# Cross-attention in turns of four heads, with the program's ends in another form

## The chip, the cores and the metric

The kernel runs on one core of one Trainium2 chip. A core has a matrix engine (PE; its weight loads are listed apart as PEld), a vector engine (DVE), an activation engine (ACT), a general engine (POOL) and a queue that issues the transfers (SP). Each takes its own instructions in the order in which the program lists them, and the engines wait for one another by semaphores. The metric is the device time of one execution in microseconds (us), lower is better.

## The reference

One decoder block on `x` of 8 sequences x 224 rows x 512, with a context of 8 x 750 x 384:

```python
# self-attention: 16 heads of 64, RMS norm in front, normed q and k, tanh soft clamp
x = layernorm(x + self_attention(x))
# cross-attention: 16 heads of 64
q = split_heads(x @ Wq); k = split_heads(context @ Wk); v = split_heads(context @ Wv)
sim = einsum('bhid,bhjd->bhij', q, k) * SCALE
out = einsum('bhij,bhjd->bhid', softmax(sim), v)
x = layernorm(x + out @ Wo + bo)
# feed-forward with ternary weights and 8-bit activations, inner width 2048
x = layernorm(x + ffn(x))
```

## The kernel before, in words

The 1792 rows of `x` lie in 14 tiles of 128 rows (`NX`). Three stages follow one another: self-attention, cross-attention, feed-forward. Inside a stage the order of each engine's instructions is written out by hand: what the program calls first, the engine does first. The change is mostly in the middle stage.

**Units.** Cross-attention is done in 64 units: 8 sequences b times 8 pairs of heads hp. For each unit:

- `scores` multiplies keys by queries (12 matmul calls into 6 PSUM tiles of 125 x 448, `sc_c`, line 1067). ACT copies each tile to SBUF (`cpT`, line 1075). DVE keeps an elementwise maximum (`cm`, line 1077), folds it once more (`cmx`, line 1081).
- `across` turns column maxima and the column sums of the unit before into rows: two transposed reductions (`mx_r`, line 1095), four small copies between partition groups (`mx_s`, line 1102), reductions and a reciprocal, three more small copies (`mx_n`, line 1124). All of it is on DVE.
- `negated_maxima` spreads the result by a transpose into a PSUM tile (`mx_b`, line 1131).
- `exponentials` subtracts the maxima on DVE (two instructions of 125 x 1344, line 1141), takes the exponential on ACT (two, line 1149) and sums on POOL (lines 1151 to 1153, into `csm`).
- `weighted` multiplies the exponentials by the values (`ov_c`, line 1161); `normalise` scales by the reciprocal sums (`rc_c`, line 1174, and line 1178) into `oT`.

**Products.** Keys and values are made for four heads at once by seven block products, `half_products` (line 244), which needs three PSUM accumulators x, z and w. Its part up to the first `yield` runs the products x, z, x, w, x; its rest runs w and x again. Between two products of one accumulator ACT has to copy the first out: `m1` (line 266), then `c11` (272), `u2` (274), `c22` (279), `u4` (282); POOL adds `m1` to `c11` and `u4` to `c22` (lines 288 and 289). The rest ends with a DVE add (`c21`, line 294) and an ACT copy (`c12`, line 298). In the trace key products bear the names `k_x`, `k_z`, `k_w` (line 1028), value products `v_x`, `v_z`, `v_w` (line 1034).

**The loop** (lines 1239 to 1290) has one round for each unit n. In a round PE does: scores of n; weighted values of n-1; the first part of the products; the queries of n+1 (`mm_q`, line 1043); the rest of the products. The products are those of values in one round and those of keys in the next. ACT does in a round: the 6 copies of scores; the five copies of the first part of the products; the copy of the queries; the two exponentials; `c12`. DVE does: the maxima, `across`, the spread, the two subtractions, `c21`, `normalise`.

**Beside it.** A generator, `weight_steps`, prepares the ternary weights of the feed-forward: ACT sums and rounds, DVE clamps, transfers through SP; nearly every unit takes one of its 38 steps. `transpose_x` makes the queries' input of the next sequence, `sum_context` the block sums of its context on POOL. `cross_finish` projects a finished tile of rows by `xattn_Wo` (`mm_co`, line 232) and adds it. `norm_at` lists at which unit the layer norm of finished tiles takes a step. All PSUM tiles but `ov_c` come from one ring of seven banks.

**The end of the program** is the last tile of the feed-forward: `contract` (16 matmuls of 128 x 512), `add` (add, statistics, one power on POOL), `store` (scaling and the transfer out).

Of the kernel before, what the change touches and what calls it, by code (L numbers as in the profile page):

```python
# [64 lines left out]
def decoder_block(ctx: ExitStack, tc: tile.TileContext, a: dict, out: bass.AP):  # L65
# [249 lines left out]
    with tc.tile_pool(name="a_sb", bufs=2) as sb, tc.tile_pool(  # L315
# [366 lines left out]

        for i in range(4):
            square(i)
# [183 lines left out]
    def quantise_x(i):  # L868

        r = quant.tile([P, DIM], F32, name="xq_r")  # L870
        nc.scalar.activation(r, x[i], AF.Identity, bias=rounder, scale=x_qs[:, i, :])
        q = quant.tile([P, DIM], BF16, name="xq_q")
        nc.scalar.activation(q, r, AF.Identity, bias=unrounder)
        xqTs[i] = quant.tile([P, KD, P], BF16, name="xqT", bufs=3)
        nc.sync.dma_start_transpose(out=xqTs[i], in_=q)

    with tc.tile_pool(name="c_sb", bufs=2, reuse_waits="tile") as sb, tc.tile_pool(
# [17 lines left out]
        csm = sb.tile([P, 2, S], F32, name="csm", bufs=1)  # L895
# [158 lines left out]
        def scores(kT, qT):  # L1054

            pT = sb.tile([CT, 2, NCT, S], F32, name="cpT")
            m2 = sb.tile([CT, 2, 2, S], F32, name="cm2", bufs=1)
# [25 lines left out]
            )  # L1083
            return pT

        def across(first, last):
# [4 lines left out]
            kinds = slice(1 if last else 0, 1 if first else 2)  # L1091

            quarter = sb.tile([P, 2, 2 * NB], F32, name="mx_r", bufs=1)
            for k, y, op in ((0, mx, ALU.max), (1, csm, ALU.add))[kinds]:
                nc.vector.tensor_reduce(
                    quarter[:, k], y.rearrange("p j (b c) -> p (j b) c", c=Q32), AX.X, op,
# [3 lines left out]
            side = sb.tile([Q32, 2, 2 * NB, P // Q32], F32, name="mx_s", bufs=1)  # L1100
# [4 lines left out]
            res = sb.tile([P, 4, NB, 1], F32, name="mx_n")  # L1105
            if not last:
                nc.vector.tensor_reduce(
                    res[:Q32, 1:3, :, 0].rearrange("p j b -> p (j b)"), side[:, 0], AX.X,
                    ALU.max, negate=True,
                )  # L1110
            if not first:
                tot = sb.tile([Q32, 2, NB], F32, name="mx_t", bufs=1)
                nc.vector.tensor_reduce(
                    tot.rearrange("p j b -> p (j b)"), side[:, 1], AX.X, ALU.add
                )
                nc.vector.reciprocal(res[:Q32, 0:4:3, :, 0], tot)
# [12 lines left out]
        def negated_maxima(res):  # L1129
# [3 lines left out]
                res[:, 1:3].rearrange("p j b o -> p (j b) o").to_broadcast([P, 2 * NB, Q32]),  # L1133
# [3 lines left out]
        def exponentials(pT, nm):  # L1137

            psum = csm[:CT]
            for j in range(2):  # L1140
# [7 lines left out]
                )  # L1148
                nc.scalar.activation(pT[:, j], pT[:, j], AF.Exp)  # L1149
# [5 lines left out]
        def weighted(hp, pT, v):  # L1155

            ov = ps_ov.tile([P, S], F32, name="ov_c")
            for ct in range(NCT):
                for j in range(2):
                    h0, hq = j * DH, (2 * hp + j) % QH  # L1160
                    nc.tensor.matmul(  # L1161
                        ov[h0 : h0 + DH, :],
                        lhsT=v[:, ct, hq * DH : (hq + 1) * DH],
                        rhs=pT[:, j, ct, :],
                        start=(ct == 0),
                        stop=(ct == NCT - 1),
                    )
            return ov

        def normalise(b, hp, ov, res):  # L1170
            rc = sb.tile([P, S], F32, name="rc_c", bufs=1)
            for j in range(2):
                half = slice(j * DH, (j + 1) * DH)
                nc.vector.transpose(
                    rc[half], res[half, 3 * j].to_broadcast([DH, NB, Q32])
                )
            c = b % 2 * S
            nc.vector.tensor_tensor(oT[:, hp, c : c + S], ov, rc, ALU.mult)
# [15 lines left out]

        norm_at = {}
        for n, i0, i1 in ((4 * NPAIR + 2, 0, 7), (7 * NPAIR + 1, 7, NX - 3)):
# [4 lines left out]
        norm_at[6 * NPAIR] = (quantise_x, 0)  # L1203
        norm_at[6 * NPAIR + 1] = (quantise_x, 1)
# [3 lines left out]
        units = [(b, hp) for b in range(B) for hp in range(NPAIR)]  # L1208
        steps = weight_steps()
        kq, vs, outs = {}, {}, {}  # L1210
# [310 lines left out]
```

## Time and profile before

| | |
|---|---|
| median of 3 runs | 1646.17 us (1645.54 to 1646.76) |
| the profiled execution | 1645.14 us, its span 1643.4 us |
| PE, PEld | busy 1623.3 us, 1147.3 us |
| DVE, ACT, POOL | busy 1336.5 us, 976.8 us, 901.4 us |
| granted PE clock | 0.999 |
| DMA queue q1 | 147.93 MB, 29.2% of 16 engines' span |
| cross-attention, first scores to first matmul of the feed-forward | 508.62 to 1491.17 us |

The span runs from the first to the last instruction; the time of the execution has some 1.7 us around it. "Busy" of PE counts matmuls whose ends are modelled and which overlap, so what a matmul costs in a dense stretch is read from the distance of starts, not from its mean duration. Matmuls of 32-bit numbers appear as two records each: the 12 calls of `scores` are 24 records. In the lists by time a line gives start, duration, engine, source line, operation, tiles and shapes, a count where alike instructions were merged, and in square brackets the engine's idle time before, with what ended it. "Pitch" below means the distance from one start to the next.

### The profile page before, as it was taken

What the parts mean: (1) busy time and instruction counts of PE and PEld (TensorE: products, weight loads), DVE (VectorE), ACT (ScalarE), POOL (GpSimd) and SP (SyncE); (2) the same over time, 40 slices, a digit from 0 to 9 for tenths busy, and PEclk for the clock granted to TensorE, in tenths of its full rate; (3) what the DMA queues carried; (4) which work ended last, traced back from release to release, by engine and by line L of the source; (5) the groups of instructions that cost most, each with busy time, mean ns of one, the idle gap of its engine ahead of it and who ended that gap; (6) DMA issues with size and microseconds to landing.
All of it is one profiled execution on the core that took longest, in us unless ns stands there. A gap on an engine that the chain in (4) does not pass through costs nothing.

```text
span 1643.4 us, 27371 instructions
## 1 busy us (share of the span) xinstructions
PE 1623.3 (99%) x9844; PEld 1147.3 (70%) x9858; DVE 1336.5 (81%) x2813; ACT 976.8 (59%) x1774; POOL 901.4 (55%) x792
## 2 busy tenths in 40 slices
PE   8999999999999999999999999999999999999998
PEld 4777666767747877876876876877877777874443
DVE  3999787878866887886986986898987787987877
ACT  4766555646515766765775775666665565655663
POOL 5785565554523665655565565565665565653244
PEclk9999999999999999999999999999999999999999
DMA  7005232312305333321332232232221131122343
GB/s 256 39 39 193 65 119 87 105 49 74 91 32 177 128 123 119 126 95 48 111 114 81 84 114 83 76 115 83 60 74 47 41 100 44 49 104 39 65 90 103
DMA packets 140071, 149.67 MB, mean 91 GB/s; under 512 B 41120, under 2 KB 106144, under 8 KB 137504
## 3 DMA queue, kind: packets, MB, share of 16 engines
q1 hardware_dynamic: 139936, 147.93, 29.2%
q8 instruction: 78, 1.28, 0.3%
q14 instruction: 57, 0.47, 0.1%
HBM read 122.47 MB, written 16.78 MB: 85 GB/s over the span
## 4 chain that ended last, share of the span: by engine, by line
PE 85%; DVE 9%; ACT 3%; issue 2%; POOL 0%; DMA 0%; POOLq 0%; SPq 0%; ACTq 0%; DVEq 0%
PE sc_c L1067 8%; PE ov_c L1161 8%; PE mm_o L629 6%; PE k_x L1028 6%; PE mm_co L232 6%; PE mm_f L1322 6%; PE v_x L1034 5%; PE mm_q L1043 5%; PE mm_v L503 5%; PE q_x L437 5%; PE k_w L1028 4%; PE v_w L1034 4%; PE ov_a L596 3%; PE sc_a L527 3%; PE q_w L437 2%; PE k_z L1028 2%
## 5 line engine op out<-in xcount | busy, mean ns | idle before, releaser
L1151 POOL TENSOR_TENSOR csh<-cpT 125x672 f32<-125x672 f32 x128 | 207.7, 1623 | 161.4 <-DVE cpT L1141 123.5
L1075 ACT COPY cpT<-sc_c 125x448 f32<-125x448 f32 x384 | 173.8, 562 | 76.3 <-PE sc_c L1067 74.8
L167 POOL TENSOR_TENSOR nm_i<-nm_q,mhalf 128x28 f32<-128x28 f32 x32 | 154.6, 4831 | 96.0 <-DVE nm_q L484 95.9
L1149 ACT ACTIVATE cpT<-cpT 125x1344 f32<-125x1344 f32 x128 | 169.1, 1323 | 48.1 <-DVE cpT L1141 40.2
L1141 DVE TENSOR_TENSOR cpT<-cpT,mx_b 125x1344 f32<-125x1344 f32 x128 | 193.2, 1550 | 2.2
L1067 PE MATMUL sc_c<-cqT,ckT 64*125 64x224 f32 x1536 | 172.5, 360 | 3.8 <-DVE cpT L1141 2.9
L1067 PEld LDWEIGHTS sc_c<-cqT,ckT 64*125 64x125 f32 x1536 | 143.1, 184 | 36.9 <-issue 22.5
L1161 PE MATMUL ov_c<-cpT,cv 125*64 125x224 f32 x1536 | 159.4, 357 | 0.0
L1161 PEld LDWEIGHTS ov_c<-cpT,cv 125*64 125x64 f32 x1536 | 104.8, 137 | 47.2 <-issue 11.2
L1077 DVE TENSOR_TENSOR cm<-sc_c,cpT 125x448 f32<-125x448 f32 x128 | 73.8, 619 | 73.9 <-ACT cpT L1075 73.9
L1043 PE MATMUL mm_q<-xT,xattn_Wq 128*128 128x224 f32 x512 | 107.3, 352 | 0.0
L1153 POOL TENSOR_TENSOR csm<-csm,csh 125x224 f32<-125x224 f32 x128 | 97.6, 763 | 10.0
L503 PE MATMUL mm_v<-wv,xnT 128*128 128x512 f32 x224 | 100.4, 592 | 0.0
L1043 PEld LDWEIGHTS mm_q<-xT,xattn_Wq 128*128 128x128 f32 x512 | 94.3, 190 | 8.1
L252 ACT ACTIVATE pr<-sc_a 128x448 f32<-128x448 f32 x120 | 57.9, 535 | 69.5 <-PE sc_a L527 69.4
L1152 POOL TENSOR_TENSOR csm<-csh 125x224 f32<-125x224 f32 x128 | 93.7, 732 | 10.0
L629 PE MATMUL mm_o<-attn_Wo,oT 128*128 128x512 f32 (+1 forms) x224 | 98.7, 594 | 0.0
L232 PE MATMUL mm_co<-xattn_Wo,coT 128*128 128x512 f32 (+1 forms) x256 | 98.6, 594 | 0.0
L1322 PE MATMUL mm_f<-ternary,xqT 128*128 128x512 bf16 x435 | 97.6, 379 | 0.7
L551 DVE TRANSPOSE_TENSOR_REDUCE sm_q<-pr 128x28 f32<-128x896 f32 x64 | 70.6, 1104 | 23.5 <-ACT pr L252 23.0
L1322 PEld LDWEIGHTS <-xqT 128*128 128x128 bf16 x448 | 43.8, 98 | 53.2 <-issue 0.6
L232 PEld LDWEIGHTS mm_co<-xattn_Wo,coT 128*128 128x128 f32 (+1 forms) x256 | 40.3, 177 | 50.6 <-issue 49.3
(211 smaller groups left out, 3723.9 us busy)
## 6 DMA issues: line engine op xcount, KB each, us to landing
xw<-w_sums SPq DMA_DIRECT2D x64, 320.0 KB, 3.0
w_slot<-qk_sums SPq DMA_DIRECT2D x22, 512.0 KB, 3.7
w_stage<-w_gateT SPq DMA_DIRECT2D x8, 1024.0 KB, 5.2
w_stage<-w_upT SPq DMA_DIRECT2D x8, 1024.0 KB, 5.3
w_stage<-w_downT SPq DMA_DIRECT2D x8, 1024.0 KB, 5.6
xw<-xattn_Wk SPq DMA_DIRECT2D x32, 192.0 KB, 2.6
xw<-xattn_Wv SPq DMA_DIRECT2D x32, 192.0 KB, 2.5
tern<-w_t SPq DMA_DIRECT2D x24, 256.0 KB, 2.0
```

The costliest lines, as they stand in the source:

```text
L232: nc.tensor.matmul(mm[row : row + m, :], lhsT=oT[:, k, at : at + m], rhs=w[:, k, :], start=(k == 0), stop=(k == NPAIR - 1),)
L503: nc.tensor.matmul(mm, lhsT=xnT[:, k, at : at + P], rhs=wv[:, k, c * 512 : (c + 1) * 512], start=(k == 0), stop=(k == KD - 1),)
L629: nc.tensor.matmul(mm[row : row + lhsT.shape[-1], :], lhsT=lhsT, rhs=wo[:, hp, :], start=(hp == 0), stop=(hp == NPAIR - 1),)
L1028: nc.tensor.matmul(mm, lhsT=w, rhs=c, start=start, stop=True, skip_group_check=True)
L1043: nc.tensor.matmul(mm, lhsT=xwq[:, k, hp * P : (hp + 1) * P], rhs=xT[:, k, :], start=(k == 0), stop=(k == KD - 1),)
L1067: nc.tensor.matmul(sc[j][:, i, :], lhsT=kT[h0 : h0 + DH, ct * CT : (ct + 1) * CT], rhs=qT[h0 : h0 + DH, :], start=True, stop=True,)
L1075: nc.scalar.copy(pT[:, j, 2 * c2 : 2 * c2 + 2, :], sc[j])
L1141: nc.vector.tensor_tensor(pT[:, j], pT[:, j], nm[:CT, j] .rearrange("p (o q) -> p o q", o=1) .to_broadcast([CT, NCT, S]), ALU.add,)
L1149: nc.scalar.activation(pT[:, j], pT[:, j], AF.Exp)
L1151: nc.gpsimd.tensor_tensor(half, pT[:, j, 0:3], pT[:, j, 3:6], ALU.add)
L1161: nc.tensor.matmul(ov[h0 : h0 + DH, :], lhsT=v[:, ct, hq * DH : (hq + 1) * DH], rhs=pT[:, j, ct, :], start=(ct == 0), stop=(ct == NCT - 1),)
L1322: nc.tensor.matmul(mm, lhsT=xqTs[i][:, k, :], rhs=w[:, k, cols], start=(k == 0), stop=(k == KD - 1),)
```

## The change

Two units make a turn of four heads. In turn d PE does: the weighted values of both units of turn d-1 side by side (one PSUM bank); the scores of both units of d; the queries of the first unit of d+1; the first part of the value products of d; the queries of the second unit; the rest of the value products; the key products of d+1. `across` is called once for four heads; the transposed reduction of the maxima has moved into `scores`, once for each unit, and that of the sums is one of double width. `negated_maxima`, the subtraction (now `less_maxima`) and the exponentials are called for each unit: those of the first between the two parts of the value products, those of the second between the two parts of the key products. One weight step is taken in a turn, and one more where a tile is finished; what is left of them follows the loop, and so does the loading of the ternary weights. At the start of the program 20 matmuls on a cleared tile are added. At its end the last tile is contracted in two halves of 256 columns, and each half is added, measured, scaled and stored by itself.

```diff
+        cleared = sb.tile([P, P], F32, name="cleared", bufs=1)
+        nc.vector.memset(cleared, 0.0)
+        warm = ps_mm.tile([P, P], F32, tag="mm", name="warm")
+        for _ in range(20):
+            nc.tensor.matmul(warm, lhsT=cleared, rhs=cleared, start=True, stop=True)
+
         for i in range(4):
             square(i)
...
-        def scores(kT, qT):
+        def scores(kT, qT, quarter):
...
             nc.vector.tensor_tensor(
                 mx[:CT], m2[:, :, 0, :], m2[:, :, 1, :], ALU.max
             )
+
+            nc.vector.tensor_reduce(
+                quarter, mx.rearrange("p j (b c) -> p (j b) c", c=Q32), AX.X, ALU.max,
+                apply_transpose=True,
+            )
             return pT
...
-            kinds = slice(1 if last else 0, 1 if first else 2)
...
+            kinds = slice(2 if last else 0, 2 if first else 4)
+            if not first:
                 nc.vector.tensor_reduce(
-                    quarter[:, k], y.rearrange("p j (b c) -> p (j b) c", c=Q32), AX.X, op,
+                    quarter[:, 2:].rearrange("p u n -> p (u n)"),
+                    csm.rearrange("p u j (b c) -> p (u j b) c", c=Q32), AX.X, ALU.add,
                     apply_transpose=True,
                 )
...
-                nc.vector.reciprocal(res[:Q32, 0:4:3, :, 0], tot)
+                for j in range(2):
+                    nc.vector.reciprocal(
+                        res[:Q32, 3 * j, :, 0].rearrange("p (u b) -> p u b", u=2), tot[:, :, j]
+                    )
...
-        def weighted(hp, pT, v):
+        def weighted(d, pTs, v):
 
-            ov = ps_ov.tile([P, S], F32, name="ov_c")
-            for ct in range(NCT):
+            ov = ps_ov.tile([P, 2, 256], F32, name="ov_c")
+            for u in range(2):
+                for ct in range(NCT):
...
+        def quantise_first(i):
+            quantise_x(
+                i,
+                sb.tile([P, 2, 2, S], F32, tag="cm2", name="xq_r", bufs=1)
+                .rearrange("p i j q -> p (i j q)")[:, :DIM],
+                sb.tile([P, PIECE], BF16, tag="w_t", name="xq_q", bufs=1)[:, :DIM],
+            )
...
+        for d in range(ND):
+            b, hp = units[2 * d]
+            more = d + 1 < ND
+            if d > 0:
+                ov = weighted(d - 1, pTs, v)
+            quarter = sb.tile([P, 4, 2 * NB], F32, name="mx_r", bufs=1)
+            pTs = [scores(kT[:, u], qTs[u], quarter[:, u]) for u in range(2)]
+            res = across(quarter, d == 0, False)
+            qTs = []
+            if more:
+                qTs.append(turn_queries(d + 1, 0))
+            v, values = turn_values(d)
+            next(values)
+            nm = negated_maxima(res, 0)
+            if more:
+                qTs.append(turn_queries(d + 1, 1))
+            less_maxima(pTs[0], nm)
+            exponentials(pTs[0], 0)
+            for _ in values:
                 pass
...
+            if d > 0:
+                normalise(d - 1, ov, res)
             for f in late:
                 f()
             late.clear()
+            if more:
+                kT, keys = turn_keys(d + 1)
+                next(keys)
+            nm = negated_maxima(res, 1)
+            less_maxima(pTs[1], nm)
+            exponentials(pTs[1], 1)
+            if more:
+                for _ in keys:
+                    pass
...
+            weight_step()
...
             if spare:
                 cross_finish(spare.pop(0))
+                for f in late:
+                    f()
+                late.clear()
+                weight_step()
...
         cross_finish(NX - 3)
...
+        cross_project(NX - 2, 0, NPAIR - 2)
+        cross_project(NX - 1, 0, NPAIR - 2)
+        ov = weighted(ND - 1, pTs, v)
+        quarter = sb.tile([P, 4, 2 * NB], F32, name="mx_r", bufs=1)
+        normalise(ND - 1, ov, across(quarter, False, True))
         for i in (NX - 2, NX - 1):
-            cross_project(i, NPAIR - 1, NPAIR)
+            cross_project(i, NPAIR - 2, NPAIR)
             cross_add(i)
...
-        def contract(i):
+        def contract(i, parts=1):
...
+            for c, dn in enumerate(dns[i]):
+                for k in range(HID // P):
+                    nc.tensor.matmul(
+                        dn,
+                        lhsT=hqT[:, k, :],
+                        rhs=wd[:, k, c * n : (c + 1) * n],
...
+        def finish_end():
+
+            _, deq = deqs.pop(END)
+            halves = [x[END][:, c : c + DIM // 2] for c in range(0, DIM, DIM // 2)]
+            st = stat.tile([P, 2, 6], F32, name="ln_st2", bufs=1)
+            for c, (y, dn) in enumerate(zip(halves, dns.pop(END))):
+                nc.vector.scalar_tensor_tensor(y, dn, deq, y, ALU.mult, ALU.add)
+                nc.vector.bn_stats(st[:, c, :], y)
+            mv, rs = ln_mv[:, END, :], ln_rs[:, END, :]
+            nc.vector.bn_aggr(mv, st)
+            nc.vector.tensor_scalar(ln_ve[:, END, :], mv[:, 1:2], LN_EPS, None, ALU.add)
+            rsqrt(rs, ln_ve[:, END, :])
+            store(nc.vector, 1)
+            for c, y in enumerate(halves):
+                nc.vector.tensor_scalar(
+                    y, y, mv[:, 0:1], rs, ALU.subtract, ALU.mult
+                )
+                nc.sync.dma_start(
+                    out=x_out[END * P :, c * DIM // 2 : (c + 1) * DIM // 2], in_=y
+                )
...
-        contract(END)
+        contract(END, 2)
         add(NX - 2)
-        add(END)
-        store(nc.vector, 2)
+        finish_end()
```

The layer norm's steps of `norm_at` move by up to two units, so that two of them fall into one turn, and the first two row tiles quantised for the feed-forward (`quantise_first`) use the rooms of `cm2` and `w_t` instead of rooms of their own.

## The prediction

> **What bounds the kernel now.** First the page's busy shares and its chain of waits:
>
> ```profile
> PE 1623.3 (99%) x9844; PEld 1147.3 (70%) x9858; DVE 1336.5 (81%) x2813; ACT 976.8 (59%) x1774; POOL 901.4 (55%) x792
> PE 85%; DVE 9%; ACT 3%; issue 2%; POOL 0%; DMA 0%; POOLq 0%; SPq 0%; ACTq 0%; DVEq 0%
> ```
>
> PE is busy all the time and is most of the chain, so the time falls only where PE's stream gets shorter, and rises with every hole in it. Then the list by time of a clean stretch of cross-attention, PE:
>
> ```profile
> 1421.60 2.54 PE L1067 MATMUL sc_c<-cqT,ckT 64*125 64x224 f32 x24
> 1424.06 2.49 PE L1161 MATMUL ov_c<-cpT,cv 125*64 125x224 f32 x24
> 1426.48 0.92 PE L1034 MATMUL v_x<-xw,ctx_odd 128*125 128x128 f32 x6
> 1431.17 1.68 PE L1043 MATMUL mm_q<-xT,xattn_Wq 128*128 128x224 f32 x8
> 1432.69 1.47 PE L1034 MATMUL v_w<-xw,ctx_odd 128*125 128x128 f32 x12
> 1435.40 1.78 PE L1067 MATMUL sc_c<-cqT,ckT 64*125 64x224 f32 x16
> ```
>
> Scores start at 1421.60 and 1435.40: 13.80 us for a unit with value products, 13.53 for one with key products, 27.34 for two. The pieces follow each other without a hole: scores 2.47, weighted values 2.42, value products 4.69 + 2.71, queries 1.51 (pitches). The first and last product records of a unit take about 0.10 more than the others: that is what a change of tile shape costs, four times in 27.34. The other two engines of the same unit, ACT and then DVE:
>
> ```profile
> 1422.71 2.72 ACT L1075 COPY cpT<-sc_c 125x448 f32<-125x448 f32 x6
> 1427.50 0.48 ACT L266 COPY cm<-v_x 125x384 f32<-125x384 f32 x1 [2.08 <-PE v_x L1034]
> 1433.14 2.72 ACT L1149 ACTIVATE cpT<-cpT 125x1344 f32<-125x1344 f32 x2
> 1435.77 0.46 ACT L298 COPY cv<-v_x 125x384 f32<-125x384 f32 x1
> 1436.51 0.97 ACT L1075 COPY cpT<-sc_c 125x448 f32<-125x448 f32 x2 [0.28 <-PE sc_c L1067]
> ```
>
> ```profile
> 1424.14 1.16 DVE L1077 TENSOR_TENSOR cm<-sc_c,cpT 125x448 f32<-125x448 f32 x2 [0.54 <-ACT cpT L1075]
> 1427.67 0.60 DVE L1095 TRANSPOSE_TENSOR_REDUCE mx_r<-csm 128x14 f32<-128x448 f32 x1
> 1428.31 0.76 DVE L1102 COPY mx_s<-mx_r 32x28 f32<-32x28 f32 x4
> 1429.72 0.98 DVE L1124 COPY mx_n<-mx_n 32x21 f32<-32x21 f32 x3
> 1430.73 0.66 DVE L1131 STREAM_TRANSPOSE mx_b<-mx_n 128x448 f32<-128x448 f32 x1
> 1431.43 3.02 DVE L1141 TENSOR_TENSOR cpT<-cpT,mx_b 125x1344 f32<-125x1344 f32 x2
> 1434.36 0.55 DVE L294 TENSOR_TENSOR cv<-v_w,cu 125x384 f32<-125x384 f32 x1
> ```
>
> ACT always waits for PE here (2.08 us before the copy of the first product), and gets to the exponentials only after the first part of the products. DVE runs without a hole from the first maximum (2.54 us after the scores start) to the end of the subtractions (10.22 us later). Exponentials (ACT goes on 1.41 us after the last subtraction), the copy of c12 and the first copies of scores close the ring in about 13.5 us: it only just fits into a unit. Where it doesn't, PE shows a hole:
>
> ```profile
> 1177.65 1.86 PE L1067 MATMUL sc_c<-cqT,ckT 64*125 64x224 f32 x14 [1.29 <-DVE cpT L1141]
> ```
>
> I went through all 64 distances between scores, less `mm_co` and the transposes: ten units (6, 7, 14, 15, 38, 39, 44 to 47) are longer than 13.53 or 13.81, by 0.8 to 2.0 us, together 13.8 us.
>
> **The turn, PE's part.** Removed: two of four changes of tile shape, 0.2 us; the matmuls stay. Without a hole a turn takes 27.14. With the first scores of a turn as zero, from the pitches above and those of the key unit before (first part 0.63, 1.26, 0.63, 1.27, 0.63): scores 2 x 2.47 and a change of shape to 5.04; queries to 6.55; first part of values 4.58, to 11.13; queries to 12.64; rest of values 2.61, to 15.25; k_x to 15.88; k_z to 17.14. There the second k_x wants to start, and it may do so only once ACT has copied the first (m1).
>
> **What stands before that copy.** ACT's order is now: 12 copies of scores, queries, five copies of the values' first part, queries, *both exponentials of the first unit*, c12 of the values, then m1 of the keys. Before, only c12 and the next scores queued behind exponentials, and the weighted values stood between. So the keys wait for DVE, whose subtractions of the first unit come after the maxima of both units and a wider `across`. Pitches, from the lines above and their neighbours: two units of maxima and folded reduction (1.07 + 1.18 + 0.71 + 0.57 each) 7.06; the sums' reduction at double width 1.10, from the same shape in self-attention:
>
> ```profile
> L551 DVE TRANSPOSE_TENSOR_REDUCE sm_q<-pr 128x28 f32<-128x896 f32 x64 | 70.6, 1104 | 23.5 <-ACT pr L252 23.0
> ```
>
> four copies 0.90 (0.80, and the 32x56 copy of self-attention is 215 ns where a clean one here is 190); two reductions 0.47 (0.12 + 0.23, each wider by about 0.06); two reciprocals 0.52; three copies 1.01; spread 0.70; subtractions 2.93. Sum 14.69. ACT has no arrears when scores start (below), so the first maximum stays at 2.54 and the subtractions end at 17.23. ACT then needs 1.41 to reach c12, 0.45 for it, 0.47 for m1, and PE takes it up some 0.06 later: 19.62. **The hole is 19.62 - 17.14 = 2.5 us in every turn.** Nothing covers it: PE keeps its order, and the next product but one needs the same accumulator.
>
> Behind it: x, w, x follow in 2.53; the second w waits for c22, whose copy ends about 0.74 after w where the x between takes 0.63 (queries stood there before), 0.1; the last two 2.52 and a change of shape bring the weighted values to 24.86 and the next scores to 29.70. **A turn takes 29.70, 2.36 more than two units.**
>
> What else was moved, and what hides it. DVE behind 17.23: c21 0.47, two transposes 1.3 (64x448, 640 ns in self-attention), the multiply 0.62 (128x448 there), spread 0.70, subtractions 2.93: 23.3. The second unit's exponentials start after u4 at 22.84 and end at 25.5; its weighted values start at 27.28, so 1.8 us of slack take in a weight clamp (0.74). POOL's sums of that unit end near 30.5, sum_context (0.92 each) or the bias (1.27) before 33, and the double reduction comes at 39. ACT ends c12 at 26.0 and has until 30.8 for a weight step (1.92 + 0.19, or 1.24 + 1.21) and a transpose copy; with a finished tile there are 6.87 us of `mm_co` more for the second step. The two norm steps in a turn (1.2 each, DVE) fall where DVE is idle, 23.9 to 32.2. The PSUM ring is read seven tiles back: the eleventh score tile waits at most 0.1 for its maximum. SP loads the block weights after their last product: 3 us to land, used over 10 us later. Ternary loads (9.2 us each) now come after the last values, with `mm_co` of 17 us and the last weighted values in front of the feed-forward. All that I cost at nothing.
>
> Bounds of the hole: the three copies take 0.56 where POOL is idle and 1.36 beside it, the four 0.80 and 1.64 (groups at 1470 and 1214 us). All clean: 2.0. All beside POOL: 3.7. I take 2.5, since POOL's add for c22 falls at 11.94 to 12.94, on the three copies, and leaves the four free. A row that I have not seen (double reduction, two-unit copies) could take another 0.8 off: 1.2 at the least.
>
> **The ends.** Warm matmuls: 40 records. In the list of the start PE is idle until 6.31; eight 128-column records then take 1.87 us, and at 11.92 eight take 1.00. If all the added ones run slow (0.234) they end near 10.5, if they turn fast after 5 us near 8. The first transposes come 1.5 to 4 late, the products behind gain about 0.9 for each eight. Between -1.0 and +1.0; I take -0.2. The last tile: adds and statistics of the second half cost 0.75 + 0.69 less, about by half, 0.6; the last scaling is two instructions of some 0.3 for one of 0.55; 32 half-width matmuls 0 to 0.3 more. Between -0.9 and +0.3; I take -0.5. The last weighted values are followed by a multiply (0.62 and a signal) that nothing covers now: +0.75. `quantise_first` shares the room of `w_t`, so ACT waits for a 2.0 us transfer in two turns: 0 to +3, I take +1.
>
> **Sum.** 31 turns with keys x 2.36 = +73.2; the last turn -0.2; the ten long units, whose ring no longer exists, -13.8; ends -0.2 - 0.5 + 0.75 + 1 = +1.05. Together +60.2 on the profiled execution's 1645.14, of which its span is 1643.4: 1705.4. The median of the runs shown is 1.0 above that execution: **1706 us**.
>
> [...] In the trace PE's longest hole in cross-attention is 1.29 us and the matmuls after it keep their pitch; after the idle start they run at half of it. [...]
> Small DVE copies double beside POOL in the rows above. [...]
>
> **Rivals.**
> - *PE never waits* (faster). One `across` for four heads relieves DVE, the ring of the ten long units is gone, and m1 is in time. It decides if DVE's 14.69 are 12.2 or less. For it: 1336.5 us of DVE busy leave room. Against: the two units' maxima and the double reduction alone are 8.2. 32 x -0.2 - 13.8 + 1.05 gives 1626 (1627 as a median): chance 0.08.
> - *A short hole*, 1.2 us: 31 x 1.06 - 13.8 + 0.85 = +20: 1666. Chance 0.12.
> - *Copies beside POOL*, hole 3.7: 31 x 3.56 - 13.8 + 0.85 = +97: 1743. For it: the long units show such copies. Chance 0.10.
> - *Half clock after the holes*: as at the start, some 5.6 us at half pace, +2.8 a turn: +87 more, 1793. Against: 1.29 us did nothing. Chance 0.04.
> - *The tile shapes cost no less*: the 0.2 stays, 1712, inside my range.
>
> **How the numbers follow.** The forecast, hole between 1.9 and 3.1, has 0.66: 1688 to 1725. 8 times in 10 the time lies between 1655 and 1745: the range takes in the bounds of the hole (1.2 gives 1666, 3.7 gives 1743), and leaves out the faster rival, the half clock and the tails of the two others. A measurement of this kernel can tell about 0.2%. Faster 0.08, same 0.01, slower 0.91.
>
> **What would show it.** PE in a turn: a hole of about 2.5 us before the second k_x, put down to ACT's copy, and distances of 29.7 between turns; ACT's m1 right behind two exponentials and c12 and no longer waiting for PE; subtractions of the first unit ending 17.2 after the scores start; no hole of scores waiting for maxima. Wrong if m1 is done before 17.14, or if DVE's first maximum of the turn comes late, which would add a second hole.

## The result and the profile after

The changed kernel takes 1738.01 us (median of 4 runs, 1736.14 to 1738.95), the kernel before beside it 1645.86 (1645.23 to 1646.76): a ratio of 1.0558, 95% interval 1.054 to 1.0576. The change costs 92 us, where 60 were forecast. The page's busy shares and chain of waits, after:

```profile
PE 1658.0 (95%) x9900; PEld 1172.4 (68%) x9914; DVE 1252.8 (72%) x2401; ACT 972.1 (56%) x1774; POOL 883.7 (51%) x792
PE 62%; DVE 20%; issue 7%; POOL 6%; ACT 5%; POOLq 0%; ACTq 0%; DVEq 0%
```

DVE's busy time fell by 84 us, as one call of `across` for four heads promises, and POOL's by 18. The time rose all the same: the span grew by 92.9 us, and of the chain PE holds 62% where it held 85%. What stands in its place is told by PE's own waits, in us in total, times, and the longest:

```profile
PE k_x L1033 <- ACT cm L266: 56.5, 30, 1.9
PE sc_c L1072 <- DVE cm L1082: 5.2, 4, 3.1
PE mm_co L232 <- DVE coT L1199: 4.3, 1, 4.3
```

None of the three was there before. The first is the hole that was forecast: before the second `k_x`, in 30 turns (0.25 us in the first, 1.93 to 1.95 in the others), waiting for ACT's copy `m1`. Here is one of the turns at full clock, from the list by time, PE, ACT and DVE in that order:

```profile
570.47 5.31 PE L1072 MATMUL sc_c<-cqT,ckT 64*125 64x224 f32 x48
575.71 1.78 PE L1048 MATMUL mm_q<-xT,xattn_Wq 128*128 128x224 f32 x8
577.33 0.82 PE L1039 MATMUL v_x<-xw,ctx_even 128*125 128x128 f32 x6
...
586.68 1.42 PE L1033 MATMUL k_z<-ctx_even,xw 128*128 128x375 f32 x4
590.04 0.90 PE L1033 MATMUL k_x<-ctx_even,xw 128*128 128x375 f32 x2 [1.94 <-ACT cm L266]
...
601.04 1.21 PE L1072 MATMUL sc_c<-cqT,ckT 64*125 64x224 f32 x10
```

```profile
586.46 2.79 ACT L1167 ACTIVATE cpT<-cpT 125x1344 f32<-125x1344 f32 x2 [2.48 <-DVE cpT L1154]
589.15 0.46 ACT L298 COPY cv<-v_x 125x384 f32<-125x384 f32 x1
589.51 0.47 ACT L266 COPY cm<-k_x 128x375 f32<-128x375 f32 x1
```

```profile
573.02 1.16 DVE L1082 TENSOR_TENSOR cm<-sc_c,cpT 125x448 f32<-125x448 f32 x2 [7.77 <-ACT cpT L1080]
584.81 3.02 DVE L1154 TENSOR_TENSOR cpT<-cpT,mx_b 125x1344 f32<-125x1344 f32 x2
587.75 0.55 DVE L294 TENSOR_TENSOR cv<-v_w,cu 125x384 f32<-125x384 f32 x1
```

ACT stands for 2.48 us before the exponentials because the subtractions come late, and then does two exponentials, `c12` and only then `m1` on which PE waits. From scores to scores this turn takes 601.04 - 570.47 = 30.57, less 0.97 of transposes 29.60; its like without transposes take 29.70.

Less the ten long units, which are gone, that accounts for some 60 us. The rest is for the most part in turns that look like this one but take 31.1 to 31.7. The turn before it, by PE, and then both turns as stretches (sums of busy time of PE, PEld, DVE, ACT and POOL; then the granted clock, DMA share and GB/s):

```profile
558.74 1.26 PE L1033 MATMUL k_x<-ctx_even,xw 128*128 128x375 f32 x2 [1.94 <-ACT cm L266]
559.80 2.71 PE L1033 MATMUL k_w<-ctx_even,xw 128*128 128x375 f32 x4
562.30 0.93 PE L1033 MATMUL k_x<-ctx_even,xw 128*128 128x375 f32 x2
```

```profile
539.17:570.47 31.30, 29.36 (x202) 23.10 (x200) 20.82 (x35) 18.32 (x32) 16.73 (x18) 0.95 0.18 48
570.47:600.07 29.60, 27.66 (x202) 22.67 (x202) 20.82 (x35) 19.36 (x35) 16.10 (x18) 1.00 0.24 76
```

The hole is the same 1.94 us, but behind it `k_w` takes 2.71 us where it takes 1.42 in the other turn, and the mean clock of the turn is 0.95. The trace's own clock records say 0.5 for exactly 3.413 us, from 559.14 on. These records change on a fixed grid of 3.413 us. Behind 11 of the 30 holes such a window follows, behind a twelfth place (1149.65) two, and two more at the end of the stage. A turn with one half-clock window is about 1.6 us longer. The four runs were granted 0.984 to 0.987 of the clock, so the number of such windows differs a little from one execution to the next.

Two further places are slow for another reason. The first maximum of some turns comes late, because DVE stands before it (DVE, then PE):

```profile
1146.71 0.55 DVE L853 TENSOR_SCALAR x<-x,ln_mvs,ln_rss 128x512 f32<-128x512 f32 x1 [10.98 <-POOL ln_rss L167]
```

```profile
1148.57 2.91 PE L1072 MATMUL sc_c<-cqT,ckT 64*125 64x224 f32 x14 [3.07 <-DVE cm L1082]
1151.41 3.35 PE L1048 MATMUL mm_q<-xT,xattn_Wq 128*128 128x224 f32 x8
```

A norm step waits 10.98 us for a power that POOL does only after the second unit's sums, and the maxima of the next turn queue behind it. And in the last turn `mm_co` waits for the last `normalise` (PE, then DVE):

```profile
1578.51 5.98 PE L232 MATMUL mm_co<-xattn_Wo,coT 128*128 128x512 f32 x8 [4.34 <-DVE coT L1199]
```

```profile
1571.52 0.69 DVE L1211 TENSOR_TENSOR x<-mm_co,x 128x512 f32<-128x512 f32 x1 [4.40 <-POOL x L1210]
1573.26 1.10 DVE L1104 TRANSPOSE_TENSOR_REDUCE mx_r<-csm 128x28 f32<-128x896 f32 x1
```

The last `across` begins only at 1573.26, behind an add that waits for POOL's bias, which itself stands behind POOL's sums.

Cross-attention, first scores to first matmul of the feed-forward, went from 982.55 to 1073.11 us. It begins 2.6 later (511.22), and 1.51 of that is only a block of queries that now stands in front. The feed-forward took 152.2 before and takes 152.0 now.

### The profile page after: what moved, and what is told of

Its sections match the earlier page's. It is cut to its first block, busy times and chain, and to the rows that moved or that the text cites. A ratio compares the mean times of both kernels' runs of the same rounds, so it can differ in the third digit from the quotient of the medians.

```text
span 1736.3 us, 26874 instructions
## 1 busy us (share of the span) xinstructions
PE 1658.0 (95%) x9900; PEld 1172.4 (68%) x9914; DVE 1252.8 (72%) x2401; ACT 972.1 (56%) x1774; POOL 883.7 (51%) x792
## 3 DMA queue, kind: packets, MB, share of 16 engines
q8 instruction: 78, 1.28, 0.3%
## 4 chain that ended last, share of the span: by engine, by line
PE 62%; DVE 20%; issue 7%; POOL 6%; ACT 5%; POOLq 0%; ACTq 0%; DVEq 0%
PE ov_c L1180 6%; PE mm_o L629 6%; PE mm_f L1378 5%; PE mm_v L503 5%; PE q_x L437 5%; PE k_w L1033 4%; PE k_x L1033 4%; PE sc_c L1072 4%; DVE cm L1082 3%; PE mm_co L232 3%; DVE cpT L1154 3%; PE ov_a L596 2%; PE sc_a L527 2%; POOL csh L1169 2%; PE mm_q L1048 2%
## 5 line engine op out<-in xcount | busy, mean ns | idle before, releaser
L288 POOL TENSOR_TENSOR cv<-cv,cm 125x384 f32<-125x384 f32 x32 | 32.0, 1001 | 303.4 <-ACT cv L272 303.4
L1072 PEld LDWEIGHTS sc_c<-cqT,ckT 64*125 64x125 f32 x1536 | 152.1, 184 | 27.2 <-DVE cm L1082 14.8
L1180 PE MATMUL ov_c<-cpT,cv 125*64 125x224 f32 x1536 | 152.2, 354 | 0.0
L1048 PE MATMUL mm_q<-xT,xattn_Wq 128*128 128x224 f32 x512 | 112.0, 363 | 0.0
L1171 POOL TENSOR_TENSOR csm<-csm,csh 125x224 f32<-125x224 f32 x128 | 90.4, 706 | 10.0
L1033 PE MATMUL k_x<-ctx_odd,xw 128*128 128x375 f32 x160 | 65.2, 506 | 29.1 <-ACT cm L266 29.1
L1033 PE MATMUL k_x<-ctx_even,xw 128*128 128x375 f32 x160 | 65.7, 510 | 27.4 <-ACT cm L266 27.4
L1170 POOL TENSOR_TENSOR csm<-csh 125x224 f32<-125x224 f32 x128 | 85.1, 665 | 10.0
```

The costliest lines, as they stand in the source:

```text
L1033: nc.tensor.matmul(mm, lhsT=w, rhs=c, start=start, stop=True, skip_group_check=True)
L1048: nc.tensor.matmul(mm, lhsT=xwq[:, k, hp * P : (hp + 1) * P], rhs=xT[:, k, :], start=(k == 0), stop=(k == KD - 1),)
L1072: nc.tensor.matmul(sc[j][:, i, :], lhsT=kT[h0 : h0 + DH, ct * CT : (ct + 1) * CT], rhs=qT[h0 : h0 + DH, :], start=True, stop=True,)
L1180: nc.tensor.matmul(ov[h0 : h0 + DH, u, :S], lhsT=v[:, ct, hq * DH : (hq + 1) * DH], rhs=pTs[u][:, j, ct, :], start=(ct == 0), stop=(ct == ...
```

## The experiments

My theory after this: the hole has the cause that was forecast (ACT's order: two exponentials and `c12` in front of `m1`), and what was missing is half clock behind holes that fill enough of one window, and POOL's queue. The rivals: the hole is DVE's or PE's own and stays when ACT's order changes; the half-clock windows come from something else (load, place) and don't follow the hole's length; the long turns are contention and not a queue. Times that follow are medians, with the ratio to the kernel before run beside it (1645.4 to 1645.9) and its interval.

**e1: the exponentials behind the keys' first part.** On the changed kernel:

```diff
-            exponentials(pTs[0], 0)
...
                 next(keys)
+            exponentials(pTs[0], 0)
             nm = negated_maxima(res, 1)
```

> The changed kernel with one edit: the first unit's exponentials are called after the first part of the key products, so ACT copies m1 before them. Theory (ACT's order makes the hole): no wait of the second k_x for m1; instead the exponentials end 23.1 after the scores start where the weighted values want 22.4, so a wait of 0.75 there; a turn 28.1 for 29.65, and since no wait is near 1.9 us the clock stays whole in the clean turns. 31 x 1.55 = 48 and some 20 of half clock: 1738 - 68 = 1670. Rival (DVE or POOL is full and sets the turn wherever the wait shows): the wait moves to the weighted values at its old size, 1735 to 1740.

Measured 1727.39, 1.0493 (1.0479 to 1.0507). The hole before `k_x` is gone and the regular turns take 27.40 to 28.04: ACT's order was its cause. But the time fell only by 11 of the 68 expected, since ten other turns (10, 13, 14, 17 to 19, 21, 25, 26, 30) now take 30 to 39 us. One of them, DVE, ACT and PE:

```profile
948.75 0.69 DVE L1211 TENSOR_TENSOR x<-mm_co,x 128x512 f32<-128x512 f32 x1 [13.51 <-POOL x L1210]
950.49 0.68 DVE L939 TENSOR_SCALAR w_stage<-w_stage 128x1024 f32<-128x1024 f32 x1
```

```profile
951.21 1.15 ACT L946 ACTIVATE w_t<-w_stage,unrounder 128x1024 bf16<-128x1024 f32 x1 [12.04 <-DVE w_stage L939]
953.39 5.28 ACT L1080 COPY cpT<-sc_c 125x448 f32<-125x448 f32 x12
```

```profile
953.96 3.95 PE L1072 MATMUL sc_c<-cqT,ckT 64*125 64x224 f32 x22 [3.82 <-ACT cpT L1080]
```

POOL's bias for a finished tile stands behind the sums of both units. With the first unit's exponentials later and the turn 2 us shorter it is done only 3.3 us after the next scores start (945.42). DVE's add waits 13.51 us for it, DVE's clamp of a weight step stands behind the add, ACT's weight step waits 12.04 for the clamp, and the copies of scores stand behind ACT's weight step. The queue that I had costed at nothing was only covered by the hole. The ten turns are some 70 us longer together: 48 of them are waits of PE in front of scores, and most of the rest is half clock, for 17 windows in these turns are at 0.5.

**e2: `c12` in front of the exponentials.** On the changed kernel:

```diff
-            exponentials(pTs[0], 0)
             for _ in values:
                 pass
+            exponentials(pTs[0], 0)
```

> The changed kernel with one edit: the rest of the value products is called before the first unit's exponentials, so c12 (0.45 us of ACT) no longer stands between them and m1. Theory (the clock halves for one window of 3.41 us when a hole of 1.93 us or more lies in one window): the hole goes from 1.94 to 1.5, a turn from 29.65 to 29.2, and no half window follows it any more. 31 x 0.45 = 14 and about 20 of half clock: 1704. Rival (the clock loses in proportion to idle time): half windows go from 12 to about 9, 1738 - 14 - 5 = 1719. Rival (m1 waits for something else than ACT's queue): 1738.

Measured 1724.26, 1.0477 (1.0463 to 1.0491). By the time alone the rival (1719) is nearer than the theory (1704); the trace decides between them. The hole is 1.56, the regular turns 29.22 to 29.32, as the theory has it, and no regular turn has a half-clock window. But turns 14, 18, 19, 26 and 30 grew to 33 to 36 by POOL's queue, as in e1, with six half-clock windows among them, and ate 20 us of the 34 expected.

**e3: a longer hole.** One more copy on ACT in front of `m1`; its result is not used:

```diff
+            delay = sb.tile([P, HALF], F32, name="delay", bufs=1)
+            nc.scalar.copy(delay, xwo[:, 0, :HALF])
```

> The changed kernel with one more ACT copy (128 x 375, about 0.46 us, of no use to the result) between c12 of the values and m1 of the keys. Theory (hole in one window): hole 2.4, a turn 30.1 at full clock, and as a longer hole lies in one window to 1.93 us or more in some 57% of the phases and not 44%, 17 or 18 half windows for 12: 31 x 0.45 + 6 x 1.7 = +24, 1762. Rival (a window must be idle as a whole, the half windows have another cause): +14, 1752, with as many half windows as before.

Measured 1740.64, 1.0587 (1.0568 to 1.0606): a miss by 21 us. The hole grew to 2.34 and the regular turns to 30.01 to 30.11, 0.4 more each, as expected. But half-clock windows occur only 8 times in the turns, not 17 or 18, and one of the 8 stands behind a wait of scores (2.68) and not behind this hole. Where the windows lie shows why: a drop followed where 2.04 us or more of a hole lay in one window, and none where the grid cut it into pieces of 1.96 or less. The holes don't meet the grid at random: four turns of a sequence, with their transposes, a finished tile and a drop, take 129.7 us here, which is 38 windows, and the first drops come back at that distance (559.40, 689.10, 818.81; in the changed kernel 559.14, 688.85, 818.56). So a longer hole can meet the grid more kindly. The 8 are those of the profiled execution (clock 0.990); the slowest of the four runs, 1747.53, had 0.986.

**e4: the ends alone.** The kernel before with the 20 warm matmuls and the last tile in halves, and nothing else of the change:

```diff
+        warm = ps_mm.tile([P, P], F32, tag="mm", name="warm")
+        for _ in range(20):
+            nc.tensor.matmul(warm, lhsT=cleared, rhs=cleared, start=True, stop=True)
...
-        contract(END)
+        contract(END, 2)
         add(NX - 2)
-        add(END)
-        store(nc.vector, 2)
+        finish_end()
```

> The kernel before with the ends of the change alone: 20 matmuls on a cleared tile at the start, the last tile contracted and stored in two halves. Theory: the start gains 0.1 (dense matmuls from 18.2 for 18.3) and the end 0.5: 0.6 us faster, ratio 0.9996. Rival (the added matmuls shift the start so that a later transfer or stage loses it again): no difference or up to 1 us slower.

Measured 1645.06 in 11 runs, 0.9996 (0.9987 to 1.0005): not to be told from no change. In the trace of the changed kernel the first dense `mm_v` starts 0.1 earlier and the end is 0.44 shorter (12.93 us from the last tile's first `dn` to the end of the span, for 13.37). But e4 also shows a wait that the kernel before doesn't have:

```profile
498.97 1.09 PE L990 MATMUL tr_x<-ident,x 128*128 128x128 f32 x8 [0.79 <-DVE x L638]
```

And its profiled execution, at 1642.31 one of its two fastest, shows something that bears on the clock:

```profile
1177.45 2.85 PE L1073 MATMUL sc_c<-cqT,ckT 64*125 64x224 f32 x14 [1.28 <-DVE cpT L1147]
```

This is the longest hole of the kernel before, 1.29 us there with the pitch kept behind it. Here, at 1.28, a half-clock window of 3.413 us follows it, from 1178.18 on. The unit becomes 1.63 us longer, but the three long units behind it (45 to 47) become 1.02, 1.17 and 1.64 shorter, so this execution gains 2.2 us by the drop. The other run at the same granted clock, 0.998, took 1642.23; the nine at 0.999 and 1.000 took 1644.6 to 1646.0.

**e5: POOL's small work first.** On the changed kernel POOL's bias, the powers of the layer norm and `sum_context` are issued at the top of the turn, in front of the sums:

```diff
+            for n in (2 * d, 2 * d + 1):
+                if n in norm_at and norm_at[n][0] is roots:
+                    roots(*norm_at[n][1:])
+            if hp in (2, 4) and b + 1 < B:
+                for i in range(2):
+                    sum_context(b + 1, hp - 2 + i)
...
+            if spare:
+                cross_bias(spare[0])
```

> The changed kernel, but POOL's small work (the bias of a finished tile, the powers of the layer norm, the context sums) is called at the top of a turn, ahead of its exponentials' sums, and no longer at its end behind them. Theory (turns 13, 14, 18, 19, 21, 26 and 30 of the changed kernel are 0.4 to 2 us longer since DVE waits for POOL's late power or bias, and ACT and the scores behind DVE): they come down to 29.65; 7.5 us and one or two half windows: 1728. The clean turns and their hole of 1.94 stay. Rival (the weight steps' own work is what these turns lack): 1738.

Measured 1732.61, 1.0529 (1.0513 to 1.0545). Every turn is now regular, 29.6 to 29.7 or 31.1 to 31.3: the long ones were POOL's queue. The gain is smaller than expected because in the new phase 16 holes, not 11, are followed by a half-clock window. Two holes of 1.94 that lay just inside a window had none, so for this hole the bound is about there. In the last turn `mm_co` waits 3.86 us, which the grid cuts into 1.97 and 1.88, and no drop follows.

**e10: e5 with `c12` first.** The edit of e2 on e5, which makes the hole 0.38 us shorter and nothing else:

```diff
-            exponentials(pTs[0], 0)
             for _ in values:
                 pass
+            exponentials(pTs[0], 0)
```

> POOL's bias, roots and context sums at the top of the turn, as in e5, and the rest of the values in front of the first unit's exponentials, as in e2. All turns are regular, and the hole before the second `k_x` falls from e5's 1.94 to 1.56 us. If a stretch at half clock follows only where about 1.93 us of a window of 3.41 us are idle, all 16 of e5 go: 1732.6 - 30 x 0.38 - 16 x 1.6 = 1696, and turns of 29.2 to 29.3 throughout. Rival: the length of the hole doesn't decide, and e2 lacked the half-clock stretches because its turns lay otherwise; then some of the 16 stay, and the time lies between 1696 and 1721.

Measured 1698.21, 1.0319 (1.0302 to 1.0336), where 1696 was expected. PE's waits of e5 and then of e10:

```profile
PE k_x L1033 <- ACT cm L266: 58.4, 31, 1.9
```

```profile
PE k_x L1033 <- ACT cm L266: 48.2, 31, 1.6
```

The waits fell by 10 us, the time by 34. All 31 turns take 29.17 to 29.34, and the 16 half-clock windows are gone. The last turn, which met the grid worse this time, is 2.5 longer, so the windows gave 34 + 2.5 - 10 = 26.5 us, 1.7 each. This is the run that shows what the clock costs here, and that for this hole, between the same key products, the length decides. e4 shows that it does not do so for every hole.

**e6: both.** The edit of e1 on e5.

> Both edits: the first unit's exponentials behind the first part of the keys, and POOL's small work at the top of the turn. In the run with the first edit alone the clean turns fell to 27.4 to 28.04, but ten turns with a finished tile or a norm step were 2 to 11 us longer, 70 us together, DVE waiting for POOL's bias (13.5 us in one) and ACT's next scores behind a weight step that waits for DVE. Theory (POOL's order makes these): they come down to 28: 1727 - 70 = 1657, and no half windows but at the end. Rival (the two units' exponentials simply end too late for two weight steps in a turn): 1700 to 1727.

Measured 1654.33, 1.0053 (1.0039 to 1.0066). With neither hole nor queue nearly all of the 92 us is gone: turns of 27.40 to 28.05, one of 28.2 and one of 28.8. What is left lies in the turns of about 28 and in the last one, where the hole of 3.86 us that cost no drop in e5 lies with 3.17 in one window and is followed by 6.83 at half clock.

**e7: the exponentials on both sides of the keys' first part.** On e6: the first exponential of unit 0 right behind `m1`, the second behind the keys' first part; the last weighted values in front of the last tile's projection, which covers their `across`:

```diff
+                kT, keys = turn_keys(d + 1, lambda: exponentials(pTs[0], 0, (0,)))
                 next(keys)
+                exponentials(pTs[0], 0, (1,))
...
-        cross_finish(NX - 3)
+        cross_project(NX - 3, 0, NPAIR)
         cross_project(NX - 2, 0, NPAIR - 2)
-        cross_project(NX - 1, 0, NPAIR - 2)
         ov = weighted(ND - 1, pTs, v)
...
+        cross_add(NX - 3)
+        cross_project(NX - 1, 0, NPAIR - 2)
```

> The changed kernel with ACT's exponentials spread: the first of unit 0 right behind m1 of the keys, the second behind the first part of the keys; POOL's small work at the top; the last weighted values and their normalising ahead of the last tile's projection. Theory: m1 is copied at 16.6 (no hole), the second exponential ends at 21.6 before the weighted values want it at 22.4, a turn takes 27.2: 1646 - 6 (two changes of tile shape less in a turn) - 14 (the ten long units) + 1 (start of the stage) + 2 (the last turn) - 0.7 (ends): 1628, faster than the kernel before by 1%. Rival (c11 and u2 of the keys, now behind an exponential, make a hole of their own): 27.2 + 0.5 to 0.9, 1645 to 1656.

Measured 1642.7, 0.9983 (0.9974 to 0.9992), short of the expected 1628. The turns are 27.40 to 27.49, five of them 27.8 to 27.9 and one 28.53. PE in a turn without a hole:

```profile
594.99 5.30 PE L1075 MATMUL sc_c<-cqT,ckT 64*125 64x224 f32 x48
600.23 1.78 PE L1051 MATMUL mm_q<-xT,xattn_Wq 128*128 128x224 f32 x8
601.84 0.82 PE L1042 MATMUL v_x<-xw,ctx_even 128*125 128x128 f32 x6
...
622.48 1.78 PE L1075 MATMUL sc_c<-cqT,ckT 64*125 64x224 f32 x16
```

This is the turn that I had as 27.14: the scores of both units take 5.24, not 5.04, and the queries behind them 1.61, not 1.51. The last turn still has a hole, and DVE shows its cause:

```profile
1479.49 2.93 DVE L1115 COPY mx_s<-mx_r 32x28 f32<-32x28 f32 x4
...
1485.77 6.76 PE L232 MATMUL mm_co<-xattn_Wo,coT 128*128 128x512 f32 x8 [2.89 <-DVE coT L1202]
```

**e8: the last three biases early.** Four small copies take 2.93 us while POOL adds three biases (3.72 us). On e7:

```diff
+            if d >= ND - 3:
+                cross_bias(NX - ND + d)
...
-        for i in range(NX - 3, NX):
-            cross_bias(i)
```

> The kernel of e7, in which POOL adds the bias to the last three tiles at the top of the last three turns instead of behind the last sums. In e7 three biases (3.72 us) lay beside the four small copies of the last `across`, which took 2.93 us, and PE stood still for 2.89 us before `mm_co`, with 6.8 us at half clock behind it. If the copies doubled because of POOL, they take 0.8 to 1.2, the hole falls to some 1.1, the half clock goes with it, and e7's 1642.7 falls by 1.8 + 3.4, to 1637.5, ratio 0.995 against the kernel before. Rival: the copies are late for another reason, then the time stays at 1642.7.

Measured 1640.41, 0.9971 (0.996 to 0.9982). The same two places:

```profile
1479.31 0.77 DVE L1115 COPY mx_s<-mx_r 32x28 f32<-32x28 f32 x4
...
1483.43 3.70 PE L232 MATMUL mm_co<-xattn_Wo,coT 128*128 128x512 f32 x8 [0.72 <-DVE coT L1202]
```

The copies take 0.77 us, the hole 0.72, and `mm_co` 3.70 for 6.76: three biases beside DVE's copies had cost 2.2 us of waiting and 3.1 of half clock. One by one, the first two copies of e7 and the biases beside them (DVE, POOL, DVE, POOL):

```profile
1479.49 1.32 DVE L1115 COPY mx_s<-mx_r 32x28 f32<-32x28 f32 x1
1479.49 1.27 POOL L1217 TENSOR_TENSOR x<-x,bo 128x512 f32<-128x512 f32 x1
1480.82 1.21 DVE L1115 COPY mx_s<-mx_r 32x28 f32<-32x28 f32 x1
1480.72 1.27 POOL L1217 TENSOR_TENSOR x<-x,bo 128x512 f32<-128x512 f32 x1
```

Each of the two lasts until 0.04 us behind the end of a bias; the other two, when POOL is done, take 0.18. In the median the gain is 2.3 where 5.2 were expected; the two profiled spans, 1644.3 and 1638.9, differ by 5.4. e7's profiled execution, 1646.23, is the slowest of its 11, at a granted clock of 0.997; three others have 0.998 and seven 0.999, so most of them met less of the half clock, and had less to gain.

**e9: e8 without the warm matmuls.**

```diff
-        warm = ps_mm.tile([P, P], F32, tag="mm", name="warm")
-        for _ in range(20):
-            nc.tensor.matmul(warm, lhsT=cleared, rhs=cleared, start=True, stop=True)
```

> The kernel of e8 without the 20 warm matmuls on a cleared tile. Their tile takes a place in the ring of PSUM banks, and every later tile stands one place further on. If that is why `tr_x` waits 0.79 us for DVE's last add of self-attention (it does so in the changed kernel and in e4, not in the kernel before), the hole is gone here and the first scores start about 0.7 us earlier; the start without warm matmuls gives 0.1 back. Time 1640.4 - 0.7 = 1639.7. Rival: the hole stays, and the time with it at 1640.5.

Measured 1639.37, 0.9961 (0.9946 to 0.9976), the fastest of all, though it can't be told from e8 by time. By the trace it can:

```profile
494.82 5.31 PE L631 MATMUL mm_o<-attn_Wo,oT 128*128 128x512 f32 x12
499.97 1.04 PE L985 MATMUL tr_x<-ident,x 128*128 128x128 f32 x8
```

The wait of 0.79 before `tr_x` is gone, and from the last start of `mm_o` to the first scores it takes 11.55 us (499.54 to 511.09) for 12.56 in e8 (498.89 to 511.45). So the tile is the cause. How it does it is read from the program: it takes a place in self-attention's ring of three PSUM banks, every later tile moves on by one, and the first transposes of cross-attention then fall on the bank that DVE still has to read.

## Why the prediction was right or wrong

**Right: the hole, its cause and the regular turn.** The chain came out nearly term by term. In the turn shown the subtractions end 17.28 us after the scores start (587.75 - 570.47; forecast 17.23), `m1` starts at 19.04 (forecast 17.23 + 1.41 + 0.45 = 19.09), PE takes up the second `k_x` at 19.57 (forecast 19.62), and the regular turn takes 29.60 to 29.70 (forecast 29.70). e1 confirms that the order on ACT is the cause, e2 that `c12` alone is worth 0.38, e3 that a longer wait goes straight into the turn. Of the copies that I had between two bounds, by pitches the four of `mx_s` took 0.91 (0.90 taken) and the three of `mx_n` 1.35 (1.01 taken), all of the slow row's 1.36; that the sum still came out is luck, for the maxima and the reciprocals took 0.30 less than forecast. The rivals of a short hole (1.2) and of all copies beside POOL (3.7) fell with this.

What a small copy loses beside POOL is seen one by one. In the turn shown the first of the three copies meets POOL's add for `c22` (DVE, then POOL):

```profile
582.77 0.93 DVE L1139 COPY mx_n<-mx_n 32x42 f32<-32x42 f32 x1
582.67 1.00 POOL L289 TENSOR_TENSOR cv<-cv,cu 125x384 f32<-125x384 f32 x1 [1.62 <-ACT cu L282]
```

It lasts until 0.04 us behind POOL's end, and the other two take 0.18. All 31 small copies of the changed kernel that take more than 0.26 us end 0.04 to 0.07 behind a POOL instruction, and all 81 of the kernel before within 0.05. So the copies don't double, as I read the groups: in 31 of the changed kernel's 66 groups one copy is held up, in none two. In the regular turns it is this add that the copy meets, as forecast, and it costs 0.75 us a turn (0.93 for 0.18).

The rival in which PE never waits fell with the 30 waits.

**Wrong, with little effect: "two of four changes of tile shape, 0.2 us".** Nothing of it is seen: without a hole a turn takes 27.40 to 27.49 where two units took 27.34, as the scores and the first queries take 0.3 more than forecast (e7). So PE wanted the second `k_x` at 17.48, not at 17.14 (`k_z` starts at 586.68, 16.21 after the scores, and its pitch is 1.27), and the hole is 2.09 by pitches, 1.94 as idle time, and not 2.5. The turn's end was right because ACT sets it. The rival of the tile shapes was right. For e7 to e9 it costs 31 x 0.3.

**Wrong: the clock at nothing behind the holes.** This is the largest part of the miss: eleven turns are longer than 29.65 by 18.0 in all, and the double window at 1149.65 gives some 3.4 more, together about 21 us. I had made the half clock a rival at 0.04 with the argument that a hole of 1.29 us did nothing. That argument was wrong twice: it says nothing of longer holes, and in e4 the same hole, at 1.28, was followed by a half-clock window. In the changed kernel the drops of this stage last 3.413 us or twice that (6.827) and begin on one grid of 3.413, and 1.93 to 1.95 us idle within one window, 57% of it, were enough.

With the idle time of PE added up in each window of cross-attention, over all twelve traces, 62 windows have 1.93 us or more, and 58 of them are followed by a drop (four with 1.94 to 1.97 are not). Of the windows with less that were not at half clock themselves, four are followed by one: 1.28 in e4 and 1.50, 1.86 and 1.88 in e2. In all four PE did scores and hardly anything else, while other windows of scores with 1.00 to 1.57 idle had no drop. So in these traces the bound of 1.93 holds for the windows of key products, where nothing up to 1.92 had a drop; for scores, which work on 64 x 125 where the key products work on 128 x 128, these traces give no sharp bound. Whether the smaller tile is the reason was not tested.

**Wrong: norm steps, sums and bias of POOL "all that I cost at nothing".** Each of them has room on its own engine, as I had counted. What I had not followed is who waits on another engine: POOL's power and bias stand behind the second unit's sums, DVE stands behind them for 7 to 11 us, and the next turn's first maximum stands behind DVE. In the changed kernel turns 14, 18, 19, 21, 26 and 30 are longer by about 6.8 in all without their clock; e5 removes this, and in e1 it is worth about 70, half clock behind the waits included. My own condition for a wrong forecast, that "DVE's first maximum of the turn comes late", is what came.

**Wrong: +0.75 for the last `normalise`.** The multiply itself is 0.62, as said. The wait was 4.34, since `across(last)` comes only behind the add that waits for POOL's bias; with the half clock behind it (`mm_co` 5.98 where e8 has 3.70) the term is about 6.6 and not 0.75.

**The ends.** -0.5 at the end was measured as -0.44. The -0.2 at the start can't be fixed: the first dense `mm_v` starts at 17.14, 18.19 and 18.44 in three traces with warm matmuls (e4, the changed kernel, e8) and at 18.30 and 19.07 in two without (before, e9). And the tile's place in PSUM's ring, shown by e4 and e9, cost 0.8 that I had not thought of; it is most of the 1.1 by which the stage starts later than one block of queries explains.

**The sum.** Forecast +60.2; behind it 21 of clock in the turns, 6.8 of POOL's queue, 5.9 of the last turn and 1.1 at the start of the stage make +95. The first turn has no sums to reduce and a small hole, -1.7, and the regular turns are some 0.05 shorter, -1.5: +92, and 92.9 is the span's difference. The +1 for `quantise_first` I could not find; it would be lost in this rest. 1738 lies in the wide range, and outside the forecast's own (1688 to 1725). That it lies in the wide one is luck: its upper end came from a hole of 3.7 us that didn't occur, and the half clock that brought the time there was left out of it.

**The ring of the ten long units.** e9 shows what the turns are worth without hole, queue and clock: -6.2 us. The -13.8 is there, but +0.1 for each of 31 turns (3.4), six turns of 27.8 to 28.1 (2.8 in all) and 1.0 before the first scores, most of it in the first 19 us, take a little over half of it back. The causes of those six turns were not looked for.

## What to carry to other kernels

Write down, for each copy that frees an accumulator, what stands before it on its engine: two exponentials in front of one copy cost some 2.1 us in each of 29 turns, and putting one exponential right behind it and the other behind the next copies made no hole. When a step looks free because its engine is idle, follow its result too: the wait was not on POOL but on DVE, two engines on from it. And count a hole on PE twice, once as time, and once as its share of a window of 3.413 us: at 1.56 us the price was the hole, at 1.94 it was nearly doubled in a third to a half of the turns.

## What the runs showed of the hardware

- PE's clock fell to half for a window of 3.413 us in 58 of the 62 cases in which 1.93 us or more of the window before were idle; in e10 the 31 holes of 1.47 to 1.58 us between key products, half of them wholly within one window, never did it. In windows of scores 1.28 us was enough once (e4), and 1.57 was not (e1).
- One such window costs 1.6 to 1.7 us in a turn that is full of matmuls. In e4 it made one unit 1.63 longer and the three behind it 3.83 shorter.
- The windows lie on a fixed grid, and this loop met it in a pattern, with drops that came back after 129.7 us, 38 windows. The same hole of 1.94 us was followed by 11 drops in one order and by 16 in another, and a hole of 2.34 by 7.
- Four DVE copies of 32x28 took 0.77 us alone and 2.93 while POOL added three tiles of 128x512: two of them lasted until a POOL add was done (1.32 and 1.21), the other two took 0.18.
- 40 zero records at the start, 7.17 us long, had the full clock granted from 6.18 us on (11.20 without them) and brought nothing that the median shows, and their PSUM tile cost a wait of 0.79 us some 490 us later.
